# Shares of 64-channel and 32-channel products in an involution, and the time at which its shifted patches are copied

## The chip, the cores and the metric

The kernel runs on one core of one Trainium2 chip. The metric is the device time of the whole kernel in microseconds (us), the median of several executions. A profiled execution gives the trace from which all durations below come.

## What is computed

The reference is a chain of four residual layers on x of shape (4, 256, 56, 56) in float32. Each one normalises x in groups of 8 channels and adds a function of it:

```python
x = x + _L0_conv_ref(_gn(x), ...)   # layer 0: involution, 7x7
x = x + _L1_conv_ref(_gn(x), ...)   # layer 1: two 3x3 convolutions
x = x + _L2_conv_ref(_gn(x), ...)   # layer 2: involution, 7x7, with batch norms and relu
x = x + _L3_conv_ref(_gn(x), ...)   # layer 3: gates from Fourier transforms
```

The change touches layers 0 and 2. An involution makes a 7x7 filter for every pixel and for each of 16 groups of 16 channels, out of the pixel itself (256 channels to 64, then 64 to 49 x 16), and applies it to the pixel's neighbourhood:

```python
kern = einsum('bchw,oc->bohw', einsum('bchw,oc->bohw', x, reduce_w), span_w)   # 49 * 16 values per pixel
out  = (kern.reshape(b, 16, 1, 49, H, W) * patches.reshape(b, 16, 16, 49, H, W)).sum(axis=3)
```

## The kernel before

The work of an involution layer goes by blocks: 4 images x 2 halves of 128 channels are 8 blocks ("units"). One block has two stages.

First, `tap_matrices` makes for each of the block's 8 groups the filters as matrices: a matmul (L593) writes to PSUM, and VectorE (L611) or ScalarE (L604) copies the result with its bias into `kt`. A matrix maps the 126 pixels of a patch (9 rows x 14 columns) to the 24 outputs of a tile (3 rows x 8 columns). The image of 56 x 56 has 19 tiles in height (the last one reaches one row beyond the image) and 7 in width; the matrices of a row outside the image are made from zeros.

Second, the loop over the 7 columns of tiles. For each column it calls `apply`, then `next_windows`, then `next_strip`:

- `apply` multiplies, for each of the 19 tiles of the column, the patch (126 pixels x channels, as weights) with the tap matrices (126 pixels x 24 outputs for each group) on TensorE (L635). `O_PARTS` says how. An entry `(ng, tys, nty, rows)` takes `ng` groups at a time, which is `ng` x 16 channels: the patch of 64 channels meets the matrices of 4 groups (96 columns), or that of 32 channels those of 2 groups (48 columns). Of the products of a channel with the matrices of 4 groups only those with its own group are wanted, so the rest is thrown away at the eviction. Products by 64 channels fill half of the array's columns, two of them one after the other fill PSUM's 128 partitions; by 32 channels there are four. Each float32 product stands in the trace as two matmuls with a weight load each, so a tile by 64 is 4 matmuls and 4 weight loads, one by 32 is 8 and 8. `tys` has the first tile of each PSUM bank, `nty` the tiles per bank, `rows` the image rows of the part.
- The eviction of a part picks each group's own products: ScalarE scales the first group's (L648 in layer 0, L650 in layer 2), VectorE adds the others with masks (L655, `ng` - 1 times), into the tile `un`. Then POOL (layer 0, L660) or VectorE (layer 2, L662) adds `un` to the image `xs`.
- `next_windows` makes the patches for the column three further on (`NXW` = 3). Seven transposes (L406, `begin_windows`) turn the strip of normalised pixels into seven patches, one for each third tile. ScalarE copies them from PSUM to `xw` (L418). The patches of the tiles between are the same pixels shifted by 42 or 84 partitions, and come as DMA copies from `xw` to `xw` (L424 and L426): for each of two shifts a top piece and a bottom piece, 252 and 126 KB, then 126 and 252 KB.
- `next_strip` normalises the next column's pixels into the one tile `strip_sb`, on POOL (L391) in layer 0 and mostly on ScalarE (L389) in layer 2.

The lines of the two parts and of the copies before:

```python
O_PARTS = ((4, (0, 5), 5, 30), (2, (10,), 9, 26))      # 10 tiles by 64 channels, 9 by 32

xw[: Q - cut, at : at + n, :]   <- xw[cut:Q, 0:n, :]        # L424, on SP
xw[Q - cut : Q, at : at + n, :] <- xw[:cut, 1 : 1 + n, :]   # L426, on SP; in layer 0 the second shift's on POOL
```

PSUM is used in pairs of banks, four pairs in turn: a column takes one for each part of `apply` and one for the transposes. The order on each engine is the order in which the program emits the instructions, and engines wait for each other by semaphores alone. Between the columns other work is put in by hand: bn_stats of the columns (L1105) and of the next image (L359), the next image's channel reduction (`bottleneck`, matmuls L469) behind every second block, and in layer 2 the gates of the previous image, whose pieces POOL computes and moves by DMA (L803 to L816).

Of the kernel before, what the change touches and what calls it, by code (L numbers as in the profile page):

```python
# [10 lines left out]
F32 = mybir.dt.float32  # L11
# [5 lines left out]
P = 128  # L17
B, C, H, W = 4, 256, 56, 56
# [15 lines left out]
TY, TX = 3, 8  # L34
QY, QX = TY + KK - 1, TX + KK - 1
Q = QY * QX
# [10 lines left out]

O_PARTS = ((4, (0, 5), 5, 30), (2, (10,), 9, 26))  # L50
NXW = 3


# [12 lines left out]
def run(g):  # L66
    for _ in g:
        pass
# [3 lines left out]
def net_kernel(  # L72
# [19 lines left out]
    nc = tc.nc  # L92
# [150 lines left out]
    def mark():  # L243
        return len(nc.cur_bb.bb.instructions)
# [54 lines left out]
    def involution_layer(layer, xin, xout, red, span, sb, xs_of, ahead=None, pending=None):  # L299

        with ExitStack() as es:
            wpool = es.enter_context(tc.tile_pool(name="iw", bufs=1))
            big = es.enter_context(tc.tile_pool(name="ibig", bufs=1))
            work = es.enter_context(tc.tile_pool(name="iwork", bufs=2))
            banks = es.enter_context(tc.tile_pool(name="banks", bufs=4, space=PSUM))

            def two_banks():

                return banks.tile([P, 2, 512], F32, name="ps")
# [62 lines left out]
            def next_strip():  # L372

                if len(strips) == len(columns):
                    return
                b, cb, tx = columns[len(strips)]
                rstd, shift = (t[:, cb : cb + 1] for t in norms[layer][b])
                st = strip_sb
                strips.append(st)
                lo, hi = max(0, tx * TX - PAD), min(W, tx * TX + TX + PAD)  # L380
                at = lo - (tx * TX - PAD)
                if at > 0:
                    nc.vector.memset(st[:, PAD : PAD + H, 0:at], 0.0)
                if at + hi - lo < QX:
                    nc.vector.memset(st[:, PAD : PAD + H, at + hi - lo : QX], 0.0)
                dst = st[:, PAD : PAD + H, at : at + hi - lo]
                img = xs_of[b, cb].rearrange("p (h w) -> p h w", w=W)[:, :, lo:hi]
                if layer == 2 and len(strips) > 2:
                    nc.scalar.activation(dst, img, AF.Identity, bias=shift, scale=rstd)  # L389
                else:  # L390
                    nc.gpsimd.tensor_scalar(dst, img, rstd, shift, ALU.mult, ALU.add)  # L391

            def window(ty):

                k, j = divmod(ty, TY)
                return (0, NSB, 2 * NSB - 1)[j] + k

            begun_windows = []

            def begin_windows():  # L400

                flat = strips[len(xws)].rearrange("p h w -> p (h w)")
                ps = two_banks().rearrange("p i n -> p (i n)")
                begun_windows.append(ps)
                for k in range(NSB):
                    nc.tensor.transpose(ps[:Q, k * P : (k + 1) * P], flat[:, k * Q : (k + 1) * Q], ident_sb)  # L406

            def next_windows():

                if len(xws) == len(columns):  # L410
                    return
                if not begun_windows:
                    begin_windows()
                ps = begun_windows.pop()
                xw = work.tile([Q, NTY, P], F32, name="xw", bufs=NXW)
                xws.append(xw)

                nc.scalar.copy(xw[:, :NSB, :], ps[:Q, : NSB * P].rearrange("q (n c) -> q n c", n=NSB))  # L418

                n = NSB - 1  # L420
                for j in range(1, TY):
                    cut = TY * QX * j
                    at = window(j)
                    nc.sync.dma_start(xw[: Q - cut, at : at + n, :], xw[cut:Q, 0:n, :])  # L424
                    eng = nc.sync if layer == 2 or j == 1 else nc.gpsimd
                    eng.dma_start(xw[Q - cut : Q, at : at + n, :], xw[:cut, 1 : 1 + n, :])  # L426


            h_of = {}
# [193 lines left out]
            def apply(b, cb, kt, tx, xw):  # L623

                img = xs_of[b, cb].rearrange("p (h w) -> p h w", w=W)
                y0 = 0
                for ng, tys, nty, rows in O_PARTS:
                    pair = two_banks()
                    nb, m = len(tys), ng * GC
                    v = pair[:, :nb, : ng * nty * TP].rearrange("p i (e n) -> p i e n", e=ng)  # L630
                    for i in range(nb):
                        for k in range(nty):
                            ty = tys[i] + k
                            for j in range(P // m):
                                nc.tensor.matmul(  # L635
                                    v[m * j : m * j + m, i, :, k * TP : (k + 1) * TP],
                                    xw[:, window(ty), m * j : m * j + m],
                                    kt[:, ng * j : ng * j + ng, :, ty * NTX + tx, :],
                                    start=True,
                                    stop=True,  # L640
                                )
                    n = rows // nb * TX
                    o = [v[:, :, e, :n] for e in range(ng)]
                    un = work.tile([P, 2, O_PARTS[0][3] // 2 * TX], F32, name="un")
                    un = un.rearrange("p i n -> p (i n)")[:, : rows * TX]
                    part = un.rearrange("p (i n) -> p i n", i=nb)
                    if layer == 0:
                        nc.scalar.mul(part, o[0], bn["par"][ng][:, 0:1])  # L648
                    else:
                        nc.scalar.activation(  # L650
                            part, o[0], AF.Identity, bias=bn["t4"][:, cb : cb + 1], scale=bn["s4"][ng][:, 0, cb : cb + 1]
                        )
                    for e in range(1, ng):
                        s = bn["par"][ng][:, e : e + 1] if layer == 0 else bn["s4"][ng][:, e, cb : cb + 1]
                        nc.vector.scalar_tensor_tensor(part, o[e], s, part, ALU.mult, ALU.add)  # L655
                    dst = img[:, y0 : y0 + rows, tx * TX : (tx + 1) * TX]
                    y0 += rows
                    u = un.rearrange("p (r x) -> p r x", x=TX)
                    if layer == 0:
                        nc.gpsimd.tensor_tensor(dst, u, dst, ALU.add)  # L660
                    else:
                        nc.vector.scalar_tensor_tensor(dst, u, 0.0, dst, ALU.max, ALU.add)  # L662


            if layer == 2:
# [292 lines left out]
            def place(hooks, g, at):  # L958

                for n in at:  # L960
                    hooks.setdefault(n, []).append(step(g))
# [4 lines left out]
            hooks0 = {}  # L966
            if layer == 0:
                place(hooks0, begin(), (1, 2, 4, 6, 7))
            else:
                since = mark()  # L970
                nc.sync.dma_start(z_sb, z2_dram)
                nc.sync.dma_start(zb_sb, zb2_dram)
                next_strip()
                run(bottleneck(0))
                hooks0[3] = list(pending[0])
                for _ in range(NXW - 1):
                    next_windows()
                    next_strip()
                hooks0[7] = [next_windows, next_strip]
            if layer == 0:  # L980
                next_strip()
                for i in range(NXW):
                    hooks0.setdefault(2 + 5 * i, []).extend((next_windows, next_strip))

            def last_column(sums):
                return lambda: sums(NTX - 1)
# [31 lines left out]
            for u, (b, cb) in enumerate(units):  # L1018
# [24 lines left out]
                if b + 1 < B:  # L1043
                    n = 16 if layer == 0 else (26, 21)[cb]
# [11 lines left out]
                kt = tap_matrices(b, cb, hooks)  # L1056

                begin_windows()

                early = [[] for _ in range(NTX)]  # L1060
# [41 lines left out]
                img = xs_of[b, cb].rearrange("p (h w) -> p h w", w=W)  # L1102

                def column_sums(tx, st=st, img=img):
                    nc.vector.bn_stats(st[:, tx, :], img[:, :, tx * TX : (tx + 1) * TX])  # L1105

                for tx in range(NTX):
                    if layer == 2 and u == len(units) - 1 and tx == NTX - 1:
                        column_sums(tx - 1)
                    for f in early[tx]:  # L1110
                        f()
                    apply(b, cb, kt, tx, xws[u * NTX + tx])
                    next_windows()
                    next_strip()
                    if tx > 0 and not (layer == 2 and u == len(units) - 1 and tx == NTX - 1):
                        column_sums(tx - 1)
                    for f in late[tx]:
                        f()
                if layer == 0 or b + 1 < B:
                    (nc.gpsimd if layer == 0 else nc.sync).dma_start(xout[b][cb], xs_of[b, cb])  # L1120
                prev = b, cb, st, column_sums
# [637 lines left out]
```

## Time and profile before

| | |
|---|---|
| median of 3 runs | 1791.4 us (1791.14 to 1792.2) |
| span of the profiled execution | 1791.4 us |
| the profiled execution's own time | the span; nothing measured lies around it |
| layer 0 | about 0 to 515 us |
| layer 1 | about 515 to 1255 us |
| layer 2, with layer 3's gates inside and after it | about 1255 to 1791 us |
| TensorE, weight loads, VectorE, ScalarE, POOL busy | 96%, 84%, 77%, 45%, 23% |
| L635, matmuls | 12544, 381.8 us busy |
| L593, matmuls | 6144, 383.2 us busy |
| L655 on VectorE, both layers | 448, 200.7 us busy |
| L426 on POOL | 56 issues, 31.5 us busy |

PE is TensorE's matmuls, PEld its weight loads (which overlap the matmuls), DVE is VectorE, ACT is ScalarE, POOL is GpSimd, SP the engine that issues most DMAs. Instructions are counted as records of the trace. "idle before <-" names what ended the wait of an engine; "issue" stands for a wait that no semaphore in the profile explains. A matmul's end is modelled, so starts are the safer reading. In a `126*64 126x96` of TensorE the first pair is the weights' rows and columns, the second the streamed data's partitions and elements.

### The profile page before, as it was taken

Reading aid. Unit: us, or ns where it says so; the run is one execution under the profiler, and the core shown is the slowest. Engines: PE = TensorE matmul, PEld = TensorE weight load, DVE = VectorE, ACT = ScalarE, POOL = GpSimd, SP = SyncE. Lnnn points to the kernel's source line nnn. Section 1 sums busy time; section 2 is a strip of 40 time slices with the busy share of each in tenths; the row PEclk is TensorE's granted clock in tenths of the full one; section 3 lists DMA queues with packets and bytes.
Section 4 is the critical chain, followed back from the end, with each engine's and each line's share of the span. In section 5 each row is a group of like instructions: output and inputs, shape, how many; then the busy total and the mean of one; then the engine's idle time right before and its main releaser. Section 6 shows DMA issues by size and latency. Waiting matters only on the chain.

```text
span 1791.4 us, 55774 instructions
## 1 busy us (share of the span) xinstructions
PE 1716.7 (96%) x24040; PEld 1507.5 (84%) x24040; DVE 1385.3 (77%) x2745; ACT 813.5 (45%) x1882; POOL 406.2 (23%) x627
## 2 busy tenths in 40 slices
PE   6999999999999999999999999999999999999998
PEld 4998988889978988898889888986888887788886
DVE  2777787767778988988898889885777778687775
ACT  2555556555533222222323132111767667567564
POOL 2224422444320000000000000001000355463572
PEclk9999999999989999999999999999999999999997
DMA  2445444633653021211111111122344567566653
GB/s 86 135 151 170 140 146 134 196 107 119 204 171 105 32 75 51 76 33 64 58 68 44 52 63 37 44 110 73 122 164 156 162 213 220 169 223 189 183 154 115
DMA packets 66003, 215.76 MB, mean 120 GB/s; under 512 B 13237, under 2 KB 20926, under 8 KB 62046
## 3 DMA queue, kind: packets, MB, share of 16 engines
q1 hardware_dynamic: 49262, 145.37, 25.9%
q0 software_dynamic: 14656, 64.77, 11.3%
q8 instruction: 190, 3.11, 0.7%
q10 hardware_dynamic: 1840, 2.05, 0.4%
q14 instruction: 55, 0.45, 0.1%
HBM read 76.30 MB, written 49.15 MB: 70 GB/s over the span
## 4 chain that ended last, share of the span: by engine, by line
PE 68%; DVE 19%; ACT 4%; DMA 4%; issue 3%; POOL 2%; SPq 1%; POOLq 0%; ACTq 0%; DVEq 0%
PE mm L1523 17%; PE ps L593 14%; PE ps L635 14%; PE mm L1441 9%; DVE kt L611 6%; PE mm L1412 5%; PE ps L406 3%; DMA xw<-xw 3%; DVE un L655 3%; PE ps L469 1%; DVE res L1516 1%; DVE xs L1375 1%; DVE st L1105 1%; ACT kt L604 1%; ACT hp L488 1%
## 5 line engine op out<-in xcount | busy, mean ns | idle before, releaser
L635 PE MATMUL ps<-kt,xw 126*32 126x48 f32 (+1 forms) x12544 | 381.8, 235 | 27.8 <-issue 12.2
L635 PEld LDWEIGHTS ps<-kt,xw 126*32 126x32 f32 (+1 forms) x12544 | 341.9, 121 | 74.5 <-issue 45.5
L593 PE MATMUL ps<-hp,z_sb 64*126 64x133 f32 x6144 | 383.2, 279 | 8.4 <-DVE kt L611 4.6
L1523 PE MATMUL mm<-v,u_sb 128*128 128x280 f32 (+1 forms) x1728 | 383.5, 383 | 1.9 <-DVE u_sb L1254 1.5
L593 PEld LDWEIGHTS ps<-hp,z_sb 64*126 64x126 f32 x6144 | 363.6, 185 | 24.4 <-DVE kt L611 6.8
L611 DVE TENSOR_TENSOR kt<-ps,zb_sb 126x798 f32<-126x798 f32 x352 | 332.9, 980 | 60.4 <-PE ps L593 49.2
L1523 PEld LDWEIGHTS mm<-v,u_sb 128*128 128x128 f32 x1728 | 326.1, 189 | 56.3 <-DVE u_sb L1254 1.9
L604 ACT ACTIVATE kt<-ps,zb_sb 126x133 f32<-126x133 f32 x960 | 280.1, 441 | 107.3 <-PE ps L593 107.3
L1441 PE MATMUL mm<-v,u_sb 128*128 128x252 f32 (+1 forms) x936 | 209.5, 384 | 0.0
L1441 PEld LDWEIGHTS mm<-v,u_sb 128*128 128x128 f32 x936 | 176.4, 189 | 30.5 <-issue 0.8
L655 DVE SCALAR_TENSOR_TENSOR un<-ps,s,un 128x240 f32<-128x240 f32 x224 | 102.6, 458 | 86.7 <-ACT un L650 79.9
L1560 POOL DMA_DIRECT2D x<-xs x24 | 13.1, 547 | 680.1 <-DVE xs L1559 426.5
L655 DVE SCALAR_TENSOR_TENSOR un<-ps,par_sb,un 128x240 f32<-128x240 f32 x224 | 98.1, 457 | 86.8 <-ACT un L648 82.3
L1508 ACT ACTIVATE res<-xs,shift,norm_sb 128x1120 f32<-128x1120 f32 (+1 forms) x24 | 30.2, 1258 | 236.3 <-DVE xs L1559 107.3
L418 ACT COPY xw<-ps 126x896 f32<-126x896 f32 x112 | 101.2, 905 | 44.0 <-PE ps L406 38.5
L406 PE MATMUL ps<-ident_sb,strip_sb 128*126 128x128 f32 x784 | 111.9, 283 | 8.4 <-POOL strip_sb L391 5.3
L660 POOL TENSOR_TENSOR xs<-un,xs 128x240 f32<-128x240 f32 x112 | 72.1, 664 | 192.2 <-DVE un L655 192.1
L648 ACT ACTIVATE un<-ps,par_sb 128x240 f32<-128x240 f32 x112 | 50.1, 448 | 122.5 <-PE ps L635 120.6
L650 ACT ACTIVATE un<-ps,bn_t,s 128x240 f32<-128x240 f32 x112 | 60.1, 537 | 94.7 <-PE ps L635 88.7
L406 PEld LDWEIGHTS ps<-ident_sb,strip_sb 128*126 128x126 f32 x784 | 85.1, 142 | 19.5 <-POOL strip_sb L391 8.3
L1412 PE MATMUL mm<-xs,u_sb 128*128 128x126 f32 (+1 forms) x792 | 98.7, 277 | 2.3 <-DVE xs L1375 1.3
L1412 PEld LDWEIGHTS mm<-xs,u_sb 128*128 128x128 f32 x792 | 94.4, 191 | 3.7 <-DVE xs L1428 1.6
(256 smaller groups left out, 1903.1 us busy)
## 6 DMA issues: line engine op xcount, KB each, us to landing
xw<-xw SPq DMA_DIRECT2D x168, 252.0 KB
xw<-xw SPq DMA_DIRECT2D x224, 126.0 KB
xw<-xw POOLq DMA_DIRECT2D x56, 252.0 KB, 4.6
xs<-x SPq DMA_DIRECT2D x24, 560.0 KB
x<-xs POOLq DMA_DIRECT2D x8, 1568.0 KB, 7.5
xs<-x SPq DMA_DIRECT2D x8, 1568.0 KB
xs<-in_x_dram SPq DMA_DIRECT2D x6, 1568.0 KB
x<-xs SPq DMA_DIRECT2D x6, 1568.0 KB
```

The costliest lines, as they stand in the source:

```text
L406: nc.tensor.transpose(ps[:Q, k * P : (k + 1) * P], flat[:, k * Q : (k + 1) * Q], ident_sb)
L418: nc.scalar.copy(xw[:, :NSB, :], ps[:Q, : NSB * P].rearrange("q (n c) -> q n c", n=NSB))
L593: nc.tensor.matmul(ps[:Q, i, k * NT : (k + 1) * NT], z_sb[i * R : (i + 1) * R, cb * GB // 2 + gp, z0 : z0 + Q], hp[i * R : (i + 1) * R, py ...
L604: nc.scalar.activation(kt[:, g0 + i, pb, :, k], ps[:Q, i, k * NT : (k + 1) * NT], AF.Identity, bias=zb_sb[:, cb * GB + g0 + i, p0 + k : p0 ...
L611: nc.vector.tensor_tensor(kt[:, g0 : g0 + 2, pb], ps[:Q, :, : PB * NT].rearrange("q i (k t) -> q i t k", k=PB), zb_sb[:, cb * GB + g0 : cb ...
L635: nc.tensor.matmul(v[m * j : m * j + m, i, :, k * TP : (k + 1) * TP], xw[:, window(ty), m * j : m * j + m], kt[:, ng * j : ng * j + ng, :, ...
L650: nc.scalar.activation(part, o[0], AF.Identity, bias=bn["t4"][:, cb : cb + 1], scale=bn["s4"][ng][:, 0, cb : cb + 1])
L655: nc.vector.scalar_tensor_tensor(part, o[e], s, part, ALU.mult, ALU.add)
L660: nc.gpsimd.tensor_tensor(dst, u, dst, ALU.add)
L1412: nc.tensor.matmul(ps[:, co * m : (co + 1) * m], u[ci][:, co * P : (co + 1) * P], v2[:, e, : n // 2, ci * WT : (ci + 1) * WT], start=(ci = ...
L1441: nc.tensor.matmul(ps, u1_sb[:, ci, dy, k, co * P : (co + 1) * P], v[:, k, dy * NB + ci : (dy + n - 1) * NB + ci + 1 : NB, :], start=(j == 0),
L1523: nc.tensor.matmul(ps, u2_sb[:, ci, dy, k, co * P : (co + 1) * P], v[:, k, dy * NB + ci : (dy + n - 1) * NB + ci + 1 : NB, :], start=(j == 0),
```

## The change

- `O_PARTS` becomes one part of 3 tiles by 64 channels (9 rows) and one of 16 tiles by 32 channels (two banks of 8 tiles, 48 rows). 9 + 48 = 57 rows, so the last part evicts one row more than the image has, and only the image's rows are added.
- `un` becomes a tile for each part, of one buffer each, in place of one tile with two buffers.
- The four copies of shifted patches all go to SP. The first is issued where all were issued before, behind L418. The other three are put off: the second and third are issued behind the first part of the next column's `apply`, the fourth behind its second part. Each of these three also waits (by a semaphore) for the last VectorE instruction that the program has emitted by then: L655 in layer 0, L662 in layer 2.
- Where windows are made ahead of the loop (in the first block's hooks and at layer 2's start), and at the end of a block's columns, outstanding copies are issued at once.

```diff
-O_PARTS = ((4, (0, 5), 5, 30), (2, (10,), 9, 26))
+O_PARTS = ((4, (0,), 3, 9), (2, (3, 11), 8, 48))
...
+            shifts = []
+
+            def last_of(engine):
+                return next(i for i in reversed(nc.cur_bb.bb.instructions) if i.engine == engine)
...
                 n = NSB - 1
-                for j in range(1, TY):
+
+                def shift(j, top):
                     cut = TY * QX * j
                     at = window(j)
-                    nc.sync.dma_start(xw[: Q - cut, at : at + n, :], xw[cut:Q, 0:n, :])
-                    eng = nc.sync if layer == 2 or j == 1 else nc.gpsimd
-                    eng.dma_start(xw[Q - cut : Q, at : at + n, :], xw[:cut, 1 : 1 + n, :])
+                    if top:
+                        nc.sync.dma_start(xw[: Q - cut, at : at + n, :], xw[cut:Q, 0:n, :])
+                    else:
+                        nc.sync.dma_start(xw[Q - cut : Q, at : at + n, :], xw[:cut, 1 : 1 + n, :])
+
+                shift(1, True)
+                shifts.extend([[lambda: shift(1, False), lambda: shift(2, True)], [lambda: shift(2, False)]])
+
+            def next_shifts(behind=False):
+
+                if not shifts:
+                    return
+                after = last_of(mybir.EngineType.DVE) if behind else None
+                for f in shifts.pop(0):
+                    f()
+                    if behind:
+                        tc.add_manual_dep(
+                            last_of(mybir.EngineType.SP),
+                            after.name,
+                            mybir.DependencyInfo(mybir.DependencyClass.Sync, mybir.DependencyReason.SCHED_ONLY),
+                            reason="paced",
+                        )
+
+            def windows_now():
+
+                next_windows()
+                while shifts:
+                    next_shifts()
...
-                    un = work.tile([P, 2, O_PARTS[0][3] // 2 * TX], F32, name="un")
-                    un = un.rearrange("p i n -> p (i n)")[:, : rows * TX]
+                    un = work.tile([P, rows * TX], F32, name=f"un{ng}", bufs=1)
...
-                    dst = img[:, y0 : y0 + rows, tx * TX : (tx + 1) * TX]
+                    real = min(rows, H - y0)
+                    dst = img[:, y0 : y0 + real, tx * TX : (tx + 1) * TX]
+                    u = un.rearrange("p (r x) -> p r x", x=TX)[:, :real]
                     y0 += rows
-                    u = un.rearrange("p (r x) -> p r x", x=TX)
                     if layer == 0:
                         nc.gpsimd.tensor_tensor(dst, u, dst, ALU.add)
                     else:
                         nc.vector.scalar_tensor_tensor(dst, u, 0.0, dst, ALU.max, ALU.add)
+                    next_shifts(True)
...
                 for _ in range(NXW - 1):
-                    next_windows()
+                    windows_now()
                     next_strip()
-                hooks0[7] = [next_windows, next_strip]
+                hooks0[7] = [windows_now, next_strip]
...
-                    hooks0.setdefault(2 + 5 * i, []).extend((next_windows, next_strip))
+                    hooks0.setdefault(2 + 5 * i, []).extend((windows_now, next_strip))
...
                     for f in late[tx]:
                         f()
+                while shifts:
+                    next_shifts()
```

## The prediction

> **What bounds the kernel now.** The page first: engine shares, then the DMA queues.
>
> ```profile
> PE 1716.7 (96%) x24040; PEld 1507.5 (84%) x24040; DVE 1385.3 (77%) x2745; ACT 813.5 (45%) x1882; POOL 406.2 (23%) x627
> ...
> q8 instruction: 190, 3.11, 0.7%
> ```
>
> TensorE is the busy engine. The last line is looked over easily: queue q8 carries instructions, 190 packets of 3.11 MB / 190 = 16.4 KB. TensorE has 24040 matmuls and 24040 weight loads; (24040 + 24040) / 190 = 253 per packet. So q8 brings TensorE its program in blocks of about 256 instructions.
>
> The change works in `apply` (L635), once for each of 7 columns x 8 blocks x 2 layers = 112 columns. Next I read the timeline of one column of layer 0, at 199 us (start, length, then engine, line, operation; the bracket is idle time before):
>
> ```profile
> 199.37 1.99 PEld L635 LDWEIGHTS ps<-kt,xw 126*64 126x64 f32 x40 [0.17 <-issue]
> 199.38 3.29 PE L635 MATMUL ps<-kt,xw 126*64 126x96 f32 x112
> ...
> 201.53 0.99 PEld L635 LDWEIGHTS ps<-kt,xw 126*32 126x32 f32 x72 [0.16 <-issue]
> ...
> 202.60 0.98 PE L406 MATMUL ps<-ident_sb,strip_sb 128*126 128x128 f32 x7
> ...
> 203.51 3.11 PEld L635 LDWEIGHTS ps<-kt,xw 126*64 126x64 f32 x112 [0.17 <-issue]
> ```
>
> See three stretches: the ten tiles by products of 64 (40 pairs of load and matmul, 1.99 us), the nine by products of 32 (72 pairs, 0.99 us), seven transposes. The next column starts at 203.51: 4.13 us per column, filled by TensorE. A tile by 64 costs 1.99 / 10 = 0.199 us, a tile by 32 costs 0.99 / 9 = 0.110 us though it has twice the instructions. In that stretch TensorE eats 144 instructions in 0.99 us, 145 per us, in the other 80 in 1.99 us, 40 per us.
>
> Then the waits. Weight loads of L635 waited 29.5 us for "issue" in layer 2 alone, 16.0 us before it. Part of that is the 0.16 us at each switch of the shape; the rest looks so, in the timeline from 1298.5:
>
> ```profile
> 1299.94 0.65 PEld L635 LDWEIGHTS ps<-kt,xw 126*32 126x32 f32 x41 [0.53 <-issue]
> ...
> 1309.64 0.45 PEld L635 LDWEIGHTS ps<-kt,xw 126*32 126x32 f32 x27 [0.88 <-issue]
> ```
>
> TensorE stands still in the middle of the fast stretch, with no semaphore to blame. Between the ends of two such stops I count instructions (stretch, its length, then busy time and count for PE and PEld):
>
> ```profile
> 1299.94:1304.47 4.53, 4.53 (x126) 3.99 (x126) 2.93 (x8) 2.81 (x4) 0.00 (x0) 1.00 0.58 169
> 1304.47:1309.64 5.17, 4.45 (x126) 3.90 (x126) 3.85 (x9) 2.92 (x4) 0.00 (x0) 1.00 0.59 185
> 328.72:333.33 4.61, 4.47 (x126) 3.92 (x126) 2.93 (x7) 1.80 (x3) 2.83 (x4) 1.00 0.70 186
> 333.33:338.09 4.76, 4.40 (x127) 3.85 (x127) 3.09 (x8) 1.80 (x3) 2.84 (x4) 1.00 0.62 180
> 1685.47:1691.05 5.58, 4.58 (x126) 3.92 (x126) 3.58 (x9) 2.92 (x4) 3.77 (x7) 1.00 0.95 257
> 1691.05:1696.18 5.13, 4.44 (x126) 3.93 (x126) 3.27 (x8) 2.92 (x4) 4.80 (x8) 1.00 0.96 247
> ```
>
> 126 + 126 and a few semaphore instructions: always one block. The stops come at block ends, so TensorE waits for its own program. A block then takes 4.53 to 5.58 us; layer 0's two average 4.69, layer 2's four 5.10, and the DMA share beside them is 0.58 to 0.96. With DMA idle a block has run in 3.38 us without a stop:
>
> ```profile
> 1287.51:1290.89 3.38, 3.38 (x126) 3.15 (x129) 2.49 (x6) 2.71 (x5) 0.00 (x0) 1.00 0.00 0
> ```
>
> So before the change a column of 224 + 14 = 238 instructions at 4.11 us uses up a block in 4.42 us: just about as fast as blocks come.
>
> [...]
>
> **Part by part.** The profiled execution's span is 1791.4 us, the median of the runs is also 1791.4, so sums on the span stand for the median.
>
> *TensorE's products.* Seven tiles change form: 7 x (0.199 - 0.110) = 0.62 us less per column; 112 x 0.62 = 70 us, if nothing else ends the column. 4.11 becomes 3.49.
>
> *TensorE's instructions.* Per column 3 x 4 + 16 x 8 = 140 pairs instead of 40 + 72 = 112: 280 + 14 = 294 instructions instead of 238; in all 112 x 56 = 6272, some 24 more blocks. 294 instructions in 3.49 us would need a block every 3.04 us, less than the fastest seen. This is what I hold to decide.
>
> *Evictions.* L655 takes 468 ns for 240 elements and 427 for 208, 1.28 ns per element: 72 elements about 253, 384 about 652. Per column 3 x 253 + 652 = 1411 instead of 3 x 468 + 427 = 1831 ns: VectorE is freed of 47 us in all, off the path while TensorE ends the column. ScalarE (L648 462 and 434 ns, 0.88 per element: 315 + 588) and the additions (L660 698 and 629: 335 + 992; L662 alike) stay within 10 ns. The larger last part arrives some 0.5 us later, so the strip on POOL follows later; hidden as long as a column takes over about 3.7 us (0.59 on ScalarE, 0.65 on VectorE, 0.99 for the addition, 1.0 for the strip, and four hand-overs of some 0.13 us, an estimate from the gaps in the same timeline). The row 56 that is now computed is not added: nothing. Separate buffers for the two parts have the distance that two alternating buffers had: nothing.
>
> *Copies.* The same four per column, 252 + 126 + 126 + 252 KB. In layer 0 56 issues leave POOL (563 ns each, and 27 us in which it waited for L418) and go to SP, whose issue takes 0.785 us: 4 x 0.785 = 3.1 us of SP per column, under the column's time. POOL's strip held up the transposes for 6.5 us in layer 0; I credit 3. The second and third copy now wait for VectorE's last instruction (L655, in layer 2 L662) of the next column's first part, the fourth for the end of its second part. The first copy of the next windows is queued behind that fourth one on SP, and loads of blocks and weights too; TensorE waits for all of them two or three columns later. In time: first copy about 1.1 us into a column, next two at about 2.2 to 3, the fourth 0.6 to 1.3 us into the column after, after which the next first one follows at once. With 0.8 us for each issue that is still nearly a row of four, not three separated bursts. I therefore bound a block's time from both sides: 3.4 us (idle DMA) to 4.69 and 5.10 (as measured). A longer column has DMA pauses, so I take 4.4 in layer 0 and 4.7 in layer 2.
>
> *Sum by stage.* Seven columns have 7 x 280 + 6 x 14 = 2044 instructions, 7.98 blocks; one is there already; the pieces before the first and after the last boundary take some 1.9 us. At 4.4: 6.98 x 4.4 + 1.9 = 32.6 us, against 28.2 now (190.8 to 219.0): +4.4, for four blocks of layer 0: +17.6. Where the bottleneck's long matmuls (L469, few instructions, much time) lie between columns the refills catch up: +1.5 for three, +4.5; the last block of layer 0 +3. In layer 2, 6.98 x 4.7 + 1.9 = 34.7 against 29.9, 32.9, 33.5, 31.6 and 33.0 now (first to last L635 of each block): on average +2.5, five times: +12.5. Three with the bottleneck spread over columns of 5.8 us: 310 / 256 x 4.7 = 5.7, no change. Sum 17.6 + 4.5 + 3 + 12.5 - 3 = +34.6, so about **1826 us**.
>
> **Rivals.**
> 1. *Refills bound the columns* (above): 1826. At the measured 4.69 and 5.10: +6.4 x 4, +3 x 3, +4, +5.3 x 5, +2 x 3 = 71, so 1862. Against it: only few columns of layer 0 show a stop today.
> 2. *Pacing speeds up refills.* If a fetch no longer stands behind two copies, a block may take 3.6 us in layer 0 and 3.9 in layer 2: 27.0 (-1.2) x 4, -2.5 x 3, -1, 29.1 (-3) x 5, -3 x 3 = -37: 1754. It decides where a block takes under 256 / 294 x 4.11 = 3.6 us. For it: 3.38 at idle DMA. Against: SP's own issue time spaced the copies already.
> 3. *The whole product gain*: 1791 - 70 = 1722. It asks for blocks in 3.04 us; no stretch shows it.
> 4. *Late copies.* "DMA xw<-xw" already stopped L635's matmuls 8 times in layer 2 for 8.9 us. The last copy is now issued a column nearer to its use; where output and gate traffic lengthen landings, 0.5 to 1 us for some 25 columns is 12 to 25 us on top of the first: 1840 to 1880.
>
> **How the numbers follow.** Refills as I size them 0.60, with late copies on top 0.11: both slower. Pacing helps 0.20, full gain 0.04: faster. Gain and loss cancel to within 0.2% (3.6 us, about what a measurement here can tell from no change) 0.05. The range leaves out the full gain and the far end: 1755 to 1882. The slower cases' own range is 1800 to 1882.
>
> **What would show it.** q8 near 214 packets. Weight loads of L635 by 32 with "issue" idle over 150 us instead of 45.5; stops in nearly every column, 256 instructions apart, 4.2 to 4.9 us. L655's means 253 and 652 ns, VectorE some 47 us less busy, POOL without L426. Columns of layer 0 near 4.9 us instead of 4.11. Wrong, if columns come every 3.5 to 4.0 us with blocks every 3.4: then rival 2 or 3; or if "DMA xw<-xw" is the largest wait of L635: then rival 4.

## The result and the profile after

The changed kernel takes 1833.5 us (median of 4 runs, 1831.2 to 1840.1) against 1791.8 us: a ratio of 1.0229, 95% interval 1.0201 to 1.0256. It is slower, 7.5 us above the predicted 1826. The span of its profiled execution is 1831.0 us, 39.6 more than before. Every ratio below is against executions of the kernel before that were made beside it (medians 1791.8 to 1796.9 us), so differences between runs are taken from the ratios. One execution of the first run below took 2385 us at a mean granted clock of 0.65, the others of that run 1847 to 1869 us at 0.96 to 0.97; it is left out of the ratio.

The two groups of the products before (count, then busy time, mean ns of one, idle time before them, and what ended most of it):

```profile
L635 PE MATMUL ps<-kt,xw 126*32 126x48 f32 (+1 forms) x12544 | 381.8, 235 | 27.8 <-issue 12.2
L635 PEld LDWEIGHTS ps<-kt,xw 126*32 126x32 f32 (+1 forms) x12544 | 341.9, 121 | 74.5 <-issue 45.5
```

The page of the changed kernel, engine shares, the queue that carries instructions, and the same two groups (their line is L666 now):

```profile
PE 1672.3 (91%) x27176; PEld 1452.1 (79%) x27176; DVE 1352.7 (74%) x2745; ACT 808.8 (44%) x1882; POOL 379.8 (21%) x571
...
q8 instruction: 214, 3.51, 0.8%
...
L666 PE MATMUL ps<-kt,xw 126*32 126x48 f32 (+1 forms) x15680 | 330.3, 226 | 106.5 <-issue 93.4
L666 PEld LDWEIGHTS ps<-kt,xw 126*32 126x32 f32 (+1 forms) x15680 | 280.4, 117 | 159.2 <-issue 128.5
```

The product gain is there: matmuls of the products are busy 330.3 us instead of 381.8, TensorE 44 us less in all. But it is idle for longer than that. "issue" before the weight loads has gone from 45.5 to 128.5 us, before the matmuls from 12.2 to 93.4 (the two overlap in part). q8 has brought 214 blocks instead of 190.

Where that wait lies is seen in the weight loads of two columns of layer 0, in the timeline (start, length, operation, count, and in brackets the idle time before):

```profile
203.50 0.59 PEld L666 LDWEIGHTS ps<-kt,xw 126*64 126x64 f32 x12 [0.17 <-ACT un L678]
204.24 0.99 PEld L666 LDWEIGHTS ps<-kt,xw 126*32 126x32 f32 x71 [0.15 <-issue]
206.25 0.81 PEld L666 LDWEIGHTS ps<-kt,xw 126*32 126x32 f32 x57 [1.02 <-issue]
207.14 0.75 PEld L411 LDWEIGHTS ps<-ident_sb,strip_sb 128*126 128x126 f32 x7
208.05 0.60 PEld L666 LDWEIGHTS ps<-kt,xw 126*64 126x64 f32 x12 [0.17 <-ACT un L678]
208.81 0.76 PEld L666 LDWEIGHTS ps<-kt,xw 126*32 126x32 f32 x50 [0.15 <-issue]
210.66 1.08 PEld L666 LDWEIGHTS ps<-kt,xw 126*32 126x32 f32 x78 [1.09 <-issue]
211.82 0.74 PEld L411 LDWEIGHTS ps<-ident_sb,strip_sb 128*126 128x126 f32 x7
212.73 0.39 PEld L666 LDWEIGHTS ps<-kt,xw 126*64 126x64 f32 x8 [0.17 <-ACT un L678]
```

Each of the two columns stops once in its fast stretch, after 71 loads, then after 50. From one end of a stop to the next the counts are again one block (stretch, its length, then busy time and count of matmuls, weight loads, VectorE, ScalarE and POOL; the last three figures are the granted clock, the DMA share and the GB/s moved):

```profile
201.96:206.25 4.29, 3.42 (x126) 2.87 (x127) 2.46 (x6) 1.71 (x3) 2.37 (x4) 1.00 0.48 138
206.25:210.66 4.41, 3.47 (x126) 2.92 (x127) 2.58 (x7) 1.71 (x3) 1.99 (x3) 1.00 0.55 170
210.66:214.95 4.29, 3.41 (x127) 2.86 (x127) 2.24 (x6) 1.71 (x3) 1.93 (x3) 1.00 0.53 165
214.95:219.79 4.84, 3.41 (x126) 2.87 (x127) 2.79 (x8) 1.71 (x3) 2.55 (x4) 1.00 0.59 174
```

In the second of them the trace has 126 matmuls and 126 loads up to the next stop's end, and four semaphore instructions of TensorE (three at L666, one at L411): 256. TensorE is busy for about 3.4 us of each of these blocks and gets one every 4.3 to 4.8. The columns start at 203.50, 208.05 and 212.73: 4.6 us each, where they took 4.1.

The fetch itself is in the trace. In the second of these stretches, 206.25 to 210.66, the instruction queue moves one packet:

```profile
q8 instruction: 1, 0.02, 2.1%
```

By the trace's record it has 16384 bytes, starts at 207.79, ends at 209.23, and the loads go on at 210.66, 1.43 us later. There are 49 blocks between two stops of more than 0.3 us in this trace (24 in layer 0, 25 in layer 2). Each of them has exactly one such packet, which ends 1.1 to 1.6 us before the loads go on. In 82 of the 112 columns the loads stop for more than 0.3 us with no semaphore to blame; before the change it was 28.

### The profile page after: what moved, and what is told of

It is laid out like the page before. It is cut to its first block, busy times and chain, and to the rows that moved or that the text cites. A ratio compares the mean times of both kernels' runs of the same rounds, so it can differ in the third digit from the quotient of the medians.

```text
span 1831.0 us, 62078 instructions
## 1 busy us (share of the span) xinstructions
PE 1672.3 (91%) x27176; PEld 1452.1 (79%) x27176; DVE 1352.7 (74%) x2745; ACT 808.8 (44%) x1882; POOL 379.8 (21%) x571
## 4 chain that ended last, share of the span: by engine, by line
PE 72%; DVE 14%; issue 8%; DMA 3%; ACT 3%; POOL 1%; SPq 0%; ACTq 0%; DVEq 0%; POOLq 0%
PE mm L1557 19%; PE ps L666 14%; PE ps L624 14%; PE mm L1475 10%; DVE kt L642 5%; PE mm L1446 5%; PE ps L411 4%; DMA xw<-xw 2%; PE ps L500 2%; DVE un L685 1%; DVE res L1550 1%; DVE xs L1409 1%; DVE st L1137 1%; ACT hp L519 1%; PE ps L750 1%
## 5 line engine op out<-in xcount | busy, mean ns | idle before, releaser
L666 PE MATMUL ps<-kt,xw 126*32 126x48 f32 (+1 forms) x15680 | 330.3, 226 | 106.5 <-issue 93.4
L666 PEld LDWEIGHTS ps<-kt,xw 126*32 126x32 f32 (+1 forms) x15680 | 280.4, 117 | 159.2 <-issue 128.5
L685 DVE SCALAR_TENSOR_TENSOR un<-ps,s,un 128x72 f32<-128x72 f32 x224 | 83.6, 373 | 122.4 <-ACT un L680 118.1
L685 DVE SCALAR_TENSOR_TENSOR un<-ps,par_sb,un 128x72 f32<-128x72 f32 x224 | 82.5, 371 | 117.2 <-ACT un L678 112.9
L411 PE MATMUL ps<-ident_sb,strip_sb 128*126 128x128 f32 x784 | 117.5, 291 | 12.9 <-issue 9.3
L691 POOL TENSOR_TENSOR xs<-un,xs 128x72 f32<-128x72 f32 x112 | 74.3, 663 | 236.3 <-DVE un L685 232.9
L423 ACT COPY xw<-ps 126x896 f32<-126x896 f32 x112 | 101.4, 906 | 41.9 <-PE ps L411 25.1
L678 ACT ACTIVATE un<-ps,par_sb 128x72 f32<-128x72 f32 x112 | 50.5, 453 | 146.5 <-PE ps L666 136.7
L680 ACT ACTIVATE un<-ps,bn_t,s 128x72 f32<-128x72 f32 x112 | 60.0, 539 | 116.8 <-PE ps L666 116.3
L411 PEld LDWEIGHTS ps<-ident_sb,strip_sb 128*126 128x126 f32 x784 | 88.9, 147 | 26.8 <-issue 12.6
L149 POOL TENSOR_TENSOR norm_sb<-norm_sb,mhalf 128x1 f32<-128x1 f32 x32 | 19.8, 620 | 376.0 <-DVE norm_sb L148 376.0
```

The source lines that it names most:

```text
L666: nc.tensor.matmul(v[m * j : m * j + m, i, :, k * TP : (k + 1) * TP], xw[:, window(ty), m * j : m * j + m], kt[:, ng * j : ng * j + ng, :, ...
L680: nc.scalar.activation(part, o[0], AF.Identity, bias=bn["t4"][:, cb : cb + 1], scale=bn["s4"][ng][:, 0, cb : cb + 1])
```

## The experiments

Two theories go into them. Theory 1: TensorE waits for its own program, and the number of instructions decides. Theory 2: the copies, put off and queued behind VectorE, come late. A third reading, that products by 32 channels are slow in themselves, is tried beside.

**One half of the change each.** The first run has the new shares and `un`, and the copies where they were:

```diff
-O_PARTS = ((4, (0, 5), 5, 30), (2, (10,), 9, 26))
+O_PARTS = ((4, (0,), 3, 9), (2, (3, 11), 8, 48))
```

> The new shares of products, with the copies issued as before (all four at once, the fourth by POOL in layer 0). Theory 1 (TensorE waits for its own program, a block of 256 instructions at a time): the instructions are those of the changed kernel, so 1820 to 1850 us, q8 at 214 packets, over 120 us of issue waits before L635's loads. Theory 2 (the loss comes from the copies being late or queued behind VectorE): the product gain of 70 us appears, 1720 to 1760 us.

Measured: a ratio of 1.0324 (1.0264 to 1.0385), span 1850.4 us, 214 blocks, 141.3 us of issue waits before the loads. The shares alone bring the loss, and more of it than the whole change. Theory 2 expected a gain. Blocks of layer 0, between the ends of stops:

```profile
208.03:213.13 5.10, 3.49 (x126) 2.88 (x126) 2.48 (x6) 1.71 (x3) 3.87 (x6) 1.00 0.70 183
213.13:217.15 4.02, 3.46 (x126) 2.96 (x126) 2.27 (x6) 1.71 (x3) 1.56 (x3) 1.00 0.49 146
217.15:222.78 5.63, 3.42 (x127) 2.86 (x127) 2.90 (x9) 1.71 (x3) 3.80 (x6) 1.00 0.70 184
222.78:227.88 5.10, 3.42 (x127) 2.88 (x127) 2.46 (x6) 1.71 (x3) 2.11 (x3) 1.00 0.46 118
```

The second run is the changed kernel with the old `O_PARTS`.

> The old shares of products with the copies in three portions. Theory 1: the instructions are those of before, so no loss; 1780 to 1795 us, some gain if a block's fetch meets fewer copies. Theory 2: the loss is here, 1815 us or more, with more time waited for the copies.

Measured: 1821.1 us, 1.0135 (1.0110 to 1.0161), with the same 190 blocks as before. Here theory 2 is right. Its waits, of matmuls and of weight loads (us in total, times, longest):

```profile
PE ps L666 <- DMA xw<-xw: 45.1, 35, 4.5
...
PEld ps L666 <- DMA xw<-xw: 13.8, 9, 3.7
```

These are 58.9 us of waits for copies. The kernel before had 18.9:

```profile
PE ps L635 <- DMA xw<-xw: 11.7, 11, 2.2
...
PEld ps L635 <- DMA xw<-xw: 7.2, 5, 1.8
```

So either half costs something, by different means, and the two do not add: the changed kernel's own waits for copies are 11.0 + 2.7 us. A reading that fits, though no run tests it alone, is that its columns wait for instructions long enough for the copies to land: in the kernels that put copies off in three portions, the waits for them are 8.1, 13.7, 27.9 and 58.9 us with 148, 140, 132 and 112 pairs of load and matmul per column (the first and the third follow).

**More and fewer tiles by 64.** If TensorE's own time decided, each tile moved to 32 channels would help; if instructions do, it would hurt.

```diff
-O_PARTS = ((4, (0,), 3, 9), (2, (3, 11), 8, 48))
+O_PARTS = ((4, (0,), 1, 3), (2, (1, 10), 9, 54))
```

> The changed kernel with one tile by 64 channels and eighteen by 32: 148 pairs of load and matmul per column instead of 140, and 2 x 0.09 us less of TensorE's own time. Theory 1: 16 more instructions in 112 columns are 7 more blocks of about 4.7 us, so about 1865 us. If TensorE's own time decides: 20 us less, about 1813 us.

Measured: 1865.0 us, 1.0367 (1.0343 to 1.0391), 221 blocks. By the ratios that is about 25 us above the changed kernel for 7 blocks, 3.5 us per block: Theory 1's direction, less than its 4.7. A part of it can be the clock, whose mean was 0.955 instead of 0.975; at most that is 1867.3 x 0.045 - 1831.0 x 0.025 = 38 us of TensorE's time, so the size proves little.

```diff
-O_PARTS = ((4, (0,), 3, 9), (2, (3, 11), 8, 48))
+O_PARTS = ((4, (0,), 5, 15), (2, (5, 12), 7, 42))
```

> The changed kernel with five tiles by 64 channels and fourteen by 32: 132 pairs per column, 2 x 0.09 us more of TensorE's own time. Theory 1: 7 blocks fewer, about 1800 us. If TensorE's own time decides: 20 us more, about 1853 us.

Measured: 1825.6 us, 1.0155 (1.0130 to 1.0180), 207 blocks. The direction is Theory 1's, the size less than half of it: by the ratios 13 us instead of 33. The waits for copies rise to 22.1 + 5.8 us, and the blocks of layer 0 between two stops take longer, 4.55 us on average (22 blocks) instead of 4.30 (24). How much each makes was not separated.

**Without the copies.** Both kernels with every tile taking the unshifted patch of its three, and no copy at all (the lines that issue them go too):

```diff
-                return (0, NSB, 2 * NSB - 1)[j] + k
+                return ty // TY
```

> The changed kernel without the copies of shifted patches: every tile takes the unshifted patch of its three, so two tiles in three are multiplied with the wrong pixels; instructions of TensorE are the same. Theory 1: with idle DMA a block takes about 3.4 us, a column 294 / 256 x 3.4 = 3.9 us; eight plain stages of 25.6 us instead of about 33, so about 1740 us, and faster than the kernel before without its copies. If TensorE is slow at many small products in itself, the issue waits stay at over 120 us and the time at over 1800 us.

> The kernel before without the copies, in the same way. Theory 1: columns at TensorE's own 4.1 us, nearly no issue wait beside the switch of the shape, no wait for the copies: about 1760 us, above the changed kernel without its copies by some 20 us or more. If the copies cost TensorE nothing: 1790 us.

Measured: 1768.5 us for the changed kernel (0.9861, 0.9807 to 0.9915) and 1760.6 for the one before (0.9817, 0.9763 to 0.9871). The second is as expected; the first is 28 us over its number, and not the faster of the two. Its blocks tell why:

```profile
198.49:201.98 3.49, 3.44 (x127) 2.89 (x127) 2.08 (x7) 1.71 (x3) 1.70 (x4) 1.00 0.02 5
201.98:205.42 3.44, 3.43 (x128) 2.89 (x128) 2.30 (x7) 1.71 (x3) 1.95 (x3) 1.00 0.02 5
205.42:209.11 3.69, 3.40 (x127) 2.87 (x127) 2.44 (x7) 1.71 (x3) 2.27 (x4) 1.00 0.02 4
...
1526.46:1530.62 4.16, 2.42 (x127) 2.21 (x128) 2.80 (x7) 1.23 (x3) 3.63 (x6) 1.00 0.34 114
```

With DMA idle (a share of 0.02) these blocks still take 3.44 to 3.69 us, and one in layer 2, whose other transfers go on, 4.16. Over all blocks between two stops the mean is 3.72 in layer 0 (19 blocks). 294 instructions at 3.54, the mean of the three, are 294 / 256 x 3.54 = 4.07 us per column: hardly less than the 4.11 that the old shares need on TensorE alone. Issue waits before the loads are still 90.3 us, against 26.1 in the other kernel without copies. Copies lengthen the blocks of layer 0, from 3.72 to 4.30 us on average in the changed kernel; but even without them these shares have nothing to win.

**Which part of the new order helps the new shares.** The changed kernel is some 17 us faster than the shares alone. Two things differ: the put-off, and layer 0's fourth copy, which went from POOL's queue to SP's. In the first run's kernel:

```diff
-                    eng = nc.sync if layer == 2 or j == 1 else nc.gpsimd
+                    eng = nc.sync
```

> The new shares of products, the four copies at once, all on SP (layer 0's fourth copy no longer on POOL). It separates the two things that the new order of copies does to the new shares. If putting the copies off is what helped by some 27 us: about 1860 us, as with the shares alone. If the move from POOL to SP helped: about 1835 us, as the changed kernel, with layer 0's blocks of instructions near 4.3 us instead of 4.7.

Measured: 1836.9 us, 1.0228 (1.0192 to 1.0264), the changed kernel's ratio. Issue waits before the loads are 128.3 us instead of 141.3. Two blocks of layer 0:

```profile
439.99:444.18 4.19, 3.44 (x127) 2.89 (x128) 2.14 (x7) 1.71 (x3) 3.41 (x8) 1.00 0.59 178
444.18:448.90 4.72, 3.42 (x126) 2.89 (x126) 2.40 (x7) 1.71 (x3) 3.23 (x7) 1.00 0.56 171
```

They lie at another place of layer 0 than the blocks of the first run that are shown above, so the averages over all blocks between two stops are the safer comparison: 4.21 us (26 blocks) against the first run's 4.84 (27) in layer 0, and 4.93 against 4.90 in layer 2, where the queues are the same. So the queue is what helped, and putting copies off does nothing measurable for the new shares. The same line in the kernel before:

> The kernel before with layer 0's fourth copy on SP instead of POOL, nothing else. If the 24 us that the three portions cost with the old shares come from putting the copies off: 1785 to 1797 us here. If they come from SP's queue, which is then the longer one: about 1808 us, with layer 0's matmuls waiting for copies.

Measured: 1787.2 us, 0.9957 (0.9940 to 0.9974). It beats both kernels. The same kernel once more:

> The old shares with layer 0's fourth copy on SP, once more, in more rounds: 7 us faster than before if the first measurement holds, a ratio of 0.995 to 0.997.

Measured: 1784.4 us, 0.9951 (0.9938 to 0.9965). The waits for copies are 5.1 + 0.2 us in the first of these two runs and 8.9 + 2.3 in the second. The loss of the three portions with the old shares thus comes from the put-off, and is larger than it looked: the ratios 1.0135 and 0.9957 are about 32 us apart.

**Two portions instead of three.** All three later copies behind the next column's first part:

```diff
-shifts.extend([[lambda: shift(1, False), lambda: shift(2, True)], [lambda: shift(2, False)]])
+shifts.append([lambda: shift(1, False), lambda: shift(2, True), lambda: shift(2, False)])
```

> The old shares, the second, third and fourth copy all put off behind the next column's first part, none behind its second. If the fourth copy, issued a column before its use, is what comes late: waits for copies fall from 59 us to under 30 and the time to about 1800 us. If putting off as such is the cost: about 1820 us, as with three portions.

> The changed kernel with the same two portions. Its columns are long enough that the fourth copy is in time (11 us of waits in all), so no gain there: 1825 to 1840 us. If the spacing of the copies is what eases the fetches of instructions, two portions are worse than three: 1845 us or more.

Measured: 1822.4 us (1.0153, 1.0116 to 1.0190) and 1833.6 us (1.0208, 1.0180 to 1.0237). The first expectation missed: the waits for copies stay at 42.1 + 16.5 us. So it is not the place of the fourth copy alone: all three behind the first part cost as much. Which of the three come late was not separated. The second held: with the new shares, three portions, two, or all at once give the same time.

**Fewer instructions for the same products.** The last test takes away instructions and leaves streamed columns, evictions and copies (all at once, on SP). In the part by 32, one product streams the 96 columns of two tiles through the patch of the first, so the second tile gets the wrong pixels (the main lines of the edit; the operand from `kt` changes with them):

```diff
-                        for k in range(nty):
+                        step_of = 2 if ng == 2 else 1
...
+                        for k in range(0, nty, step_of):
...
-                                    v[m * j : m * j + m, i, :, k * TP : (k + 1) * TP],
+                                    v[m * j : m * j + m, i, :, k * TP : (k + step_of) * TP],
```

> The new shares with the copies at once on SP, and the sixteen tiles by 32 channels taken two at a time: one product streams the 96 columns of two tiles through the patch of the first (the second tile so gets the wrong pixels). The streamed columns are the same, the pairs of load and matmul per column fall from 140 to 12 + 64 = 76, below the 112 of before. Theory 1 (blocks of instructions): the product gain appears and the issue waits fall to the switch of the shape, some 20 us: 1700 to 1740 us, with the waits for copies larger than before since columns take about 3.5 us. If products by 32 channels are slow in themselves: above 1790 us.

Measured: 1733.6 us, 0.9662 (0.9649 to 0.9675). Its page and one column:

```profile
q8 instruction: 158, 2.59, 0.6%
```

```profile
203.89 0.60 PEld L637 LDWEIGHTS ps<-kt,xw 126*64 126x64 f32 x12 [0.17 <-ACT un L649]
204.64 1.57 PEld L637 LDWEIGHTS ps<-kt,xw 126*32 126x32 f32 x64 [0.15 <-issue]
206.52 0.75 PEld L406 LDWEIGHTS ps<-ident_sb,strip_sb 128*126 128x126 f32 x7 [0.30 <-POOL strip_sb L391]
207.43 0.64 PEld L637 LDWEIGHTS ps<-kt,xw 126*64 126x64 f32 x12 [0.17 <-issue]
```

The column takes 3.54 us, near the 3.49 that the sum on TensorE promised. The fast stretch is 1.57 us for the same columns that take about 1.7 us in 128 pairs when nothing stops them (126 pairs in 1.72 us at 452.97 of the changed kernel), so at most some 0.2 us x 112 = 22 us of the 103 us between this run and 1836.9 are TensorE's own. The rest is waiting for the program: the issue waits before the loads fall by 83 us, from 128.3 to 45.5 (about 20 had been expected). A part of it can be the lower clock (mean 0.966 against 0.982), of which the last section tells. Those for copies are 27.0 + 6.7 us, more than before; the columns are shorter. Products by 32 channels are not slow in themselves: 1733.6 us stands against the 1790 and more that this was to show.

## Why the prediction was right, and where it was off

- **What bounds the columns.** Right: blocks of 256 instructions (the 126 + 126 + 4 counted above; over the run (27176 + 27176) / 214 = 254 matmuls and loads for each). The 214 blocks came as stated, the stops in 82 of 112 columns instead of nearly every one. Blocks between two stops take 4.30 us on average in layer 0 and 4.94 in layer 2, where 4.2 to 4.9 was stated, but single ones 3.5 to 6.8. The strongest support is the run with 76 pairs, and the packet that ends 1.1 to 1.6 us before each stop does.
- **The sum by stage.** The total came within 7.5 us in part by luck. From the first to the last product of each stage, layer 0 lost 14.6 us where 25.1 were summed (22.1 with the 3 credited to the copies), and layer 2 lost 21.8 where 12.5 were; the two errors nearly cancel. Plain stages of layer 0 were put at 32.6 us; they take 33.9, 34.5, 31.8 and 30.5, mean 32.7, but before they averaged 28.7 and not the 28.2 of the one that was read. The bottleneck's stages were put at +1.5 each; in layer 0 they came out at 35.3 us against 36.2 on average, so part of the product gain stayed. Layer 2's five plain stages were put at 34.7 and took 35.6, 3.9 more than before instead of 2.5; those with the bottleneck gained nothing and lost 0.8.
- **A block in 4.4 us in layer 0.** The figure was right (4.30), its reason was not. It was taken under the 4.69 of before because a longer column was expected to have DMA pauses. The shares alone have the longer columns too, and there a block takes 4.84 us; it is the move of the fourth copy to SP that brings 4.21.
- **Issue waits over 150 us on the loads by 32.** Mis-sized: 98.5 us there and 86.4 before the matmuls by 32. The profile splits the stops over the two.
- **The copies.** The step that credited the move from POOL to SP with 3 us, for POOL's strip, and with nothing for the fetches failed: with the new shares it makes about 17 us of difference (the ratios 1.0324 and 1.0228 differ by 0.96%, give or take 0.7), with the old ones 8 to 10. I saw SP's issue time as the price and did not see what POOL's queue cost. That the three portions are nearly a row of four held with the new shares: they change nothing there against all at once on SP.
- **Late copies.** Their mechanism was right and its place wrong. I added 12 to 25 us to the slow end; the changed kernel's waits for copies are no larger than before (13.7 us against 18.9). They are the cost with the old shares (58.9 us), whose columns are shorter.
- **Rival 2** set its point at a block in 3.6 us. Without any copies the blocks of layer 0 between two stops still take 3.72 us on average, so that spacing the copies could not reach it. That a fetch stands behind copies was an estimate, from the 3.38 us at a DMA share of 0.00 against 4.53 to 5.58 at 0.58 to 0.96; what holds a packet back beside copies was not shown.
- **The clock.** The prediction has no term for it; the last section shows that up to some 19 us of the loss can be the lower granted clock (mean 0.975 against 0.985).
- **VectorE.** Put at 47 us less, it is 32.6 us less. An L655 (L685 now) of 72 elements costs 291 ns instead of the 253 of the straight line, one of 384 costs 616 instead of 652:

```profile
L685 DVE SCALAR_TENSOR_TENSOR un<-ps,par_sb,un 128x72 f32<-128x72 f32 x168 | 48.6, 289 | 29.4 <-ACT un L678 25.3
...
L685 DVE SCALAR_TENSOR_TENSOR un<-ps,par_sb,un 128x384 f32<-128x384 f32 x56 | 34.5, 616 | 87.8 <-ACT un L678 87.6
```

Open is why a copy on POOL's queue lengthens a block more than the same copy on SP's (4.84 us against 4.21). The traces show where the time goes: in layer 0 the packet of a block starts 2.36 us after the stop before it has ended with the shares alone, 1.74 us with all copies on SP and 1.24 us without copies, while its own length (1.1 us) and the time from its end to the next load (1.35 to 1.38 us) are the same in all three. Why it starts later is not shown.

## What to carry to other kernels

Smaller products that waste less can lose when they take more instructions, as here with 140 pairs per column instead of 112 (a ratio of 1.0229): divide the records of matmuls and weight loads by the packets of the instruction queue, and look whether a stretch asks for a block faster than one has ever come (3.04 us asked, 3.38 the shortest seen before). Here a wait for "issue" in the middle of a stretch, at a distance of one block from the last, was that bound, and a product that streams more columns per instruction was worth more than one that streams fewer in all (1733.6 us with 96 columns for each product by 32, 1836.9 with 48). And a copy that is put off to keep queues clear must be priced against the shortest column that the kernel may reach, not the present one: in three portions the waits for copies were 13.7 us with 140 pairs per column and 58.9 with 112.

## What the runs showed of the hardware that I had not expected

Behind some long stops TensorE's granted clock was halved for a while. Stretches of the changed kernel, in pairs of a stop and what follows it (the granted clock is the last figure but two):

```profile
454.30:457.70 3.40, 0.81 (x44) 0.59 (x33) 0.62 (x1) 0.58 (x1) 2.02 (x6) 1.00 0.62 199
457.70:461.10 3.40, 3.40 (x65) 2.85 (x68) 1.02 (x4) 1.23 (x2) 1.59 (x4) 0.51 0.26 79
...
507.10:511.10 4.00, 0.24 (x20) 0.12 (x9) 0.00 (x0) 0.00 (x0) 0.00 (x0) 1.00 0.70 207
512.40:515.80 3.40, 3.40 (x140) 3.18 (x136) 1.83 (x6) 1.17 (x2) 2.21 (x3) 0.50 0.65 200
1717.20:1720.60 3.40, 0.17 (x11) 0.02 (x2) 0.10 (x1) 0.00 (x0) 1.84 (x3) 1.00 0.89 264
1720.70:1727.50 6.80, 6.01 (x152) 5.22 (x153) 3.33 (x7) 2.83 (x5) 6.39 (x9) 0.50 0.56 164
```

In these pairs no weight load ran for 2.72, 4.05 and 4.27 us (the first time among the seven transposes of the strip, from the end of one load at 454.97 to 457.69), and 3.4, 3.4 and 6.8 us at half the clock follow (the last from 0.8 us before the next load on). There 128 loads by 32 take 2.58 us (at 513.25), where 126 took 1.72 (at 452.97). At 280.3 the clock halved for 3.4 us behind a stop of 1.97 us that had ended at 279.70. But behind one of 3.10 us that ended at 96.96 it stayed at 1.00, so how long a stop must be was not shown. I had not counted such stops in the prediction. The mean clock of the whole run falls from 0.985 to 0.975. A long wait for instructions can thus be paid twice. At most this makes 1831.0 x 0.025 - 1791.4 x 0.015 = 19 of the 40 us, an estimate from the two mean clocks; how much it does make was not separated, since TensorE also waits less in the slow stretches: it is busy for 3.40 of 3.40, 3.40 of 3.40 and 6.01 of 6.80 us there, and for about 3.4 of 4.3 to 4.8 in the blocks of layer 0 shown first.
